# The tail of a two-layer graph kernel: the last tile's flags, the coarse trials of the left-over rows and the end of the last block, on other engines and in another order

## The chip, the cores and the metric

The kernel runs on one core of one Trainium2 chip. The core has five engines with queues of their own: TensorE (PE in the profile, its weight loads PEld), VectorE (DVE), ScalarE (ACT), GpSimd (POOL) and SyncE (SP), which here only issues transfers. Each engine takes its instructions in program order and waits for others by semaphores. The metric is the device time of one execution in microseconds; the median of three runs before the change is 1654.93 us.

## The reference

Two graph layers over 3327 nodes with 256 features, float32. Layer 0 is a graph attention layer with a GRU. Layer 1, where the change lies, runs two steps of a propagation along the adjacency and of an attention in which every row keeps only its largest probabilities, up to a sum of 0.9:

```python
def _top_p_attention(X, W1, W2, W3):
    q = X @ W1.T @ W2.T
    k = X @ W3.T
    probs = jax.nn.softmax(q @ k.T / TAU, axis=-1)
    idx = jnp.argsort(-probs, axis=-1)
    sp = jnp.take_along_axis(probs, idx, axis=-1)
    cs = jnp.cumsum(sp, axis=-1)
    keep_sorted = cs - sp < TOP_P
    mask = jnp.zeros(probs.shape, dtype=bool).at[rows, idx].set(keep_sorted)
    A = probs * mask
    return A / jnp.maximum(A.sum(-1, keepdims=True), 1e-12)

for n in range(2):
    A = _top_p_attention(Xa, W1, W2, W3)
    Xf = R @ Xf                       # R: S + identity, rows divided by their sums
    Xa = A @ Xa
    Z = Z + Xf @ U1[n].T + Xa @ U2[n].T
h = X + Z                             # then a layer norm, + X, and a second layer norm
```

## The kernel before

The rows are worked on in 26 tiles (`NT`) of 128 rows (`P`); the last one has 127 (`TAIL`). Layer 1 keeps all 3327 columns of a tile's logits and probabilities in one row of memory per node. `HALF` is 1664 columns. The second step numbers its tiles from `NT` to `2 * NT - 1`; below they are tile 0 to tile 25 of that step.

**The pipeline of the second step.** All of TensorE, ScalarE, VectorE and GpSimd run in the order in which the program issues the work. For each tile, `run` (L2387) fills seven lists of small jobs, `slots[0]` to `slots[6]`, and `product` (L2343) interleaves them with the tile's own product: group `g` of the masked probabilities is turned (`turn`, TensorE and ScalarE), multiplied (`times`, L2061 on TensorE), and then the jobs of `slots[g]` are issued. While tile `i` is multiplied, tile `i + 1` gets its list of largest probabilities (`list_1`, `list_2`), its flags (`told`), its mask (`mask`) and its neighbours' rows by gathers (`neighbour`), and earlier tiles get their row ends (`tile_end`, six steps each: ScalarE sums, three GpSimd steps, ScalarE normalising, twice over, then a store). `propagate` multiplies the neighbours (`pxf`), `h1` takes their result (ScalarE L1990, GpSimd L1991), and it is stored for later.

**Left-over rows.** A row whose short list of 32 does not settle its bound is flagged. `put_aside_1` and `put_aside_2` count flagged rows, work out a place for each with a small product on TensorE (`pos`), and scatter four numbers a row (`pay`) to a table `left_over` with an indirect DMA that GpSimd issues (L2148). Two blocks of 128 such rows, h0 and h1, are worked out again in full at the end. h0 holds rows of the first 14 tiles, h1 the rest, so h1 can be loaded (`hard_load(1)`, L2158 on SP) only when the last tile's scatter has landed. Then its indices are made (L2161 and L2162), its rows gathered (`hard_gather`, L2176), its queries and logits built (`hard_q`, `hard_exp`).

**A block's bound.** To find which probabilities to keep, a block lowers an upper bound `top` in up to six trials with the factors of `CUTS`. A trial on ScalarE (`coarse_bound`) is four passes (L2231) and eight small steps, on GpSimd; `COARSE` says how many trials of h0 and of h1 go there. A trial on VectorE (`bound`, L2258 to L2263) is one pass over all columns (`kept_sum`, L1963) and three small steps, and the rest of the six go there. Then `hard` sums what lies below `top` (L2273), finds the largest in groups (L1775), sorts a list of 72 (L1794, L1796), settles the bound (L1809 to L2295), drops up to 24 equal values in three passes over all columns (`drop`, L1957) and masks (L2301, one pass). `hard_end` makes the product (`pavh`) and starts the row end.

**The order at the end.** In the last tile's loop h0's coarse trials are finished, its VectorE work (`hard_first`) is put one step into each slot, and h1's load, queries and exponentials go between. After the loop, `ends` issues: the one coarse trial of h1; the rest of h0's work; h0's product; h1's five VectorE trials; h1's `hard`; the final check `whole` (L2523 to L2538), whose result decides if a slow version runs instead; h0's scatter; h1's product; h1's row end; h1's scatter.

Of the kernel before, what the change touches and what calls it, by code (L numbers as in the profile page):

```python
# [16 lines left out]
P = 128  # L17
# [100 lines left out]
COARSE = (4, 1)  # L118
# [1120 lines left out]
class Layer1:  # L1239
# [559 lines left out]
    def settle(self, lst, before, last, thr2, r, drop, flag, tag, room=None):  # L1799
# [19 lines left out]
        engine = nc.vector if room_given else nc.gpsimd  # L1819
# [81 lines left out]
    def list_2(self, i):  # L1901
# [8 lines left out]
            v.lst, before[:r], v.last, v.thr2, r, DROP, self.flag[:r, n, v.at : v.at + 1], tag  # L1910
# [21 lines left out]
    def one_over(self, i):  # L1932

        nc, v = self.nc, self.items[i]
        r = v.r
        nc.gpsimd.tensor_scalar(v.rA[:r], v.thr2[:r], 0.5e-12 / TOP_P, v.sA[:r], ALU.mult, ALU.max)
        nc.gpsimd.tensor_tensor(v.rA[:r], v.rA[:r], self.minus_one[:r], ALU.pow)
# [63 lines left out]
    def moments(self, src, r, tag):  # L2001

        nc = self.nc
        st = self.st.tile([P, nc.vector.BN_STATS_DIM], F32, tag="bn", name=f"bn{tag}")
        nc.vector.bn_stats(st[:r], src)
        mv = self.st.tile([P, 2], F32, tag="mv" + tag[0], name=f"mv{tag}", bufs=4)
        nc.vector.bn_aggr(mv[:r], st[:r])
        nc.gpsimd.tensor_scalar(mv[:r, 1:2], mv[:r, 1:2], 1.0, LN_EPS, ALU.mult, ALU.add)
        nc.gpsimd.tensor_tensor(mv[:r, 1:2], mv[:r, 1:2], self.power[:r], ALU.pow)
        return mv  # L2010

    def sums(self, h, r, tag):
# [7 lines left out]
        yield  # L2020
        sq = self.st.tile([P, 1], F32, tag="sq" + tag[0], name=f"sq{tag}", bufs=2)
# [7 lines left out]

    def shift(self, mv, r, tag):  # L2030
        shift = self.small("shift", f"shift{tag}")
        self.nc.gpsimd.tensor_scalar(shift[:r], mv[:r, 0:1], mv[:r, 1:2], -1.0, ALU.mult, ALU.mult)
        return shift[:r]

    def normalized(self, h, mv, shift, r):
        self.nc.scalar.activation(h, h, AF.Identity, bias=shift, scale=mv[:r, 1:2])
# [35 lines left out]
    def output_rows(self, h, terms, r, tag):  # L2072

        nc = self.nc
        m = self.moments(h, r, f"a{tag}")
        shift = self.shift(m, r, f"a{tag}")
        yield
        self.normalized(h, m, shift, r)
        nc.gpsimd.tensor_tensor(h, h, self.g[:r], ALU.mult)
        for term in terms:  # L2080
            nc.gpsimd.tensor_tensor(h, h, term, ALU.add)
# [274 lines left out]
    def ends(self, first, older, last):  # L2356
# [24 lines left out]
        for _ in self.hard_end(1):  # L2381
            pass
# [224 lines left out]
```

## Time and profile before

| what | value |
|---|---|
| median of three runs (1652.97 to 1655.37) | 1654.93 us |
| the profiled execution | 1656.51 us |
| its span in the profile | 1654.7 us |
| busy: TensorE, VectorE, ScalarE, GpSimd | 86%, 83%, 66%, 63% of the span |
| last tile's own product starts | 1505.9 us |
| h1's pay rows in hand | 1515.6 us |
| h0's first trial on VectorE | 1515.5 us |
| h1's first trial on VectorE | 1563.6 us |
| h1's list pass (L2273) | 1585.4 us |
| h1's mask (L2301) | 1618.5 us |
| h1's product on TensorE | 1623.6 to 1640.3 us |
| last scatter issued | 1649.5 us |

A line of the timeline has the start and the length in microseconds, the engine, the line of the kernel, the operation, what it writes and reads with partitions x elements, and in brackets how long the engine was idle before it and what ended that. In the view of the waits the three numbers are the total in microseconds, how often, and the longest. In the view of the windows each engine has its busy time in the window with the number of its instructions. The chain is the work that ended last, followed back from the last instruction.

### The profile page before, as it was taken

The page shows a single profiled execution, that of the slowest core. Times are in us where ns is not written, and L with a number is a line of the kernel's source. Part 1 is how long each engine was busy: PE and PEld are TensorE (multiplying, and loading weights), DVE is VectorE, ACT ScalarE, POOL GpSimd, SP SyncE. Part 2 cuts the span into 40 slices and gives each one's busy share as a digit, 9 for nine tenths or more (in the row PEclk, how much of TensorE's full clock was granted, in tenths as well). Part 3 has the DMA queues.
Part 4 walks back from the last instruction along what each step waited for, and adds up shares of the span by engine and source line. Part 5 has one row for each costly group of instructions (what it writes and reads, how often), then busy time and mean ns, then how long its engine had stood idle before and what let it go on. Part 6 is the DMA issues. An engine that isn't in the chain of part 4 may idle for free. (4 is left out here: it accounts for less than half of the span.)

```text
span 1654.7 us, 27171 instructions
## 1 busy us (share of the span) xinstructions
PE 1416.5 (86%) x7743; PEld 968.0 (59%) x7743; DVE 1367.8 (83%) x4873; ACT 1097.3 (66%) x2685; POOL 1045.5 (63%) x1523
## 2 busy tenths in 40 slices
PE   4899999986889999999988799999999999985514
PEld 3756666553555555565554477777777667664413
DVE  5799999537788888888862899999999999985992
ACT  4478888655687888788853566766766677764511
POOL 0366666604576677767753468888888878787331
PEclk7599999996799999999997899999999999997767
DMA  8977776313344344444441122222222222211000
GB/s 260 325 246 257 256 258 169 82 53 105 99 124 125 110 121 120 132 111 121 119 125 49 36 60 62 66 72 69 74 71 71 67 59 72 65 53 29 21 4 5
DMA packets 101637, 178.80 MB, mean 108 GB/s; under 512 B 25976, under 2 KB 64119, under 8 KB 101479
## 3 DMA queue, kind: packets, MB, share of 16 engines
q0 software_dynamic: 26288, 73.75, 17.4%
q1 hardware_dynamic: 61818, 93.49, 17.2%
q10 hardware_dynamic: 13372, 9.76, 1.8%
q8 instruction: 63, 1.03, 0.3%
q14 instruction: 96, 0.78, 0.2%
HBM read 139.92 MB, written 37.07 MB: 107 GB/s over the span
## 5 line engine op out<-in xcount | busy, mean ns | idle before, releaser
L2061 PE MATMUL pav<-xu,at 128*128 128x256 f32 (+2 forms) x1352 | 339.2, 396 | 21.9 <-ACT at L2047 21.9
L2061 PEld LDWEIGHTS pav<-xu,at 128*128 128x128 f32 (+2 forms) x1352 | 249.4, 194 | 114.7 <-issue 43.4
L1762 ACT COPY array<-pl 128x416 f32<-128x416 f32 (+3 forms) x402 | 184.1, 512 | 127.8 <-PE pl L1759 127.6
L1775 DVE MAX8 cand<-array 128x8 f32<-128x104 f32 (+5 forms) x1233 | 260.5, 286 | 9.5 <-ACT array L1762 9.1
L1759 PE MATMUL pl<-kT,qT 64*128 64x416 f32 (+3 forms) x804 | 204.4, 567 | 9.4 <-ACT array L1762 8.3
L667 POOL DMA_INDIRECT g<-x_rows,edge x130 | 137.0, 1054 | 46.1 <-issue 32.5
L667 POOL DMA_INDIRECT g<-whx,edge x130 | 135.3, 1041 | 46.9 <-issue 37.3
L2047 ACT COPY at<-pt 128x512 f32<-128x512 f32 (+2 forms) x182 | 95.4, 539 | 103.7 <-PE pt L2045 103.6
L667 POOL DMA_INDIRECT g<-y_rows,edge x130 | 137.1, 1054 | 37.0 <-issue 36.0
L1598 POOL DMA_INDIRECT g<-x1k,uidx x130 | 136.9, 1053 | 33.8 <-issue 25.0
L935 DVE FIND_INDEX8 at<-ones,array 128x8 uint32<-128x840 f32 (+1 forms) x104 | 105.9, 1027 | 0.0
L1759 PEld LDWEIGHTS pl<-kT,qT 64*128 64x128 f32 (+1 forms) x804 | 66.6, 187 | 65.6 <-issue 43.8
L1695 POOL TENSOR_TENSOR x<-x,c 128x256 f32<-128x256 f32 (+1 forms) x26 | 18.5, 714 | 84.6 <-ACT c L1690 84.6
L1656 PE MATMUL pav<-g,w 128*128 128x257 f32 (+1 forms) x260 | 64.1, 395 | 3.5 <-DVE w L1650 3.5
L1052 PE MATMUL acc<-g,m 128*128 128x258 f32 (+1 forms) x260 | 63.2, 391 | 0.0
L1986 PE MATMUL pxf<-g,m 128*128 128x256 f32 (+1 forms) x260 | 62.1, 386 | 0.0
L1052 PEld LDWEIGHTS acc<-g,m 128*128 128x128 f32 (+1 forms) x260 | 50.6, 195 | 18.4 <-issue 6.9
L1884 DVE SCALAR_TENSOR_TENSOR cand<-ec,high 128x256 f32<-128x256 f32 (+1 forms) x104 | 56.9, 547 | 2.8
L2094 POOL TENSOR_TENSOR h<-h 128x256 f32<-128x256 f32 (+1 forms) x26 | 55.3, 2127 | 2.0
L691 PE MATMUL pq<-xtq,wkqk 128*128 128x128 f32 (+1 forms) x208 | 36.0, 298 | 23.2 <-ACT xtq L683 16.1
L1656 PEld LDWEIGHTS pav<-g,w 128*128 128x128 f32 (+1 forms) x260 | 48.9, 196 | 10.7 <-DVE w L1650 4.0
L1079 PE MATMUL prz<-wih,hT 128*128 128x512 f32 (+1 forms) x104 | 52.4, 627 | 3.2 <-ACT hT L1072 1.5
(552 smaller groups left out, 3787.9 us busy)
## 6 DMA issues: line engine op xcount, KB each, us to landing
array<-in_adj_dram SPq DMA_DIRECT2D x25, 1248.0 KB
array<-in_adj_dram SPq DMA_DIRECT2D x25, 415.5 KB
members<-m SPq DMA_DIRECT2D x26, 320.0 KB
m<-members SPq DMA_DIRECT2D x26, 320.0 KB
x_rows<-x ACTq DMA_DIRECT2D x25, 128.0 KB
x1k<-x ACTq DMA_DIRECT2D x25, 128.0 KB
xb_rows<-xb SPq DMA_DIRECT2D x25, 128.0 KB
y_rows<-y SPq DMA_DIRECT2D x25, 128.0 KB
```

The costliest lines, as they stand in the source:

```text
L667: self.nc.gpsimd.indirect_dma_start(out=dst[:, b, :], out_offset=None, in_=table[:, :], in_offset=bass.IndirectOffsetOnAxis(ap=self.edge[: ...
L935: nc.vector.max_index(at[:r, g, :], self.ones8[:r], ad[:r, g, :])
L1052: nc.tensor.matmul(acc[:r, : self.WH], m[:, :r], g[:, k, :], start=(k == 0), stop=(k == EB - 1))
L1598: nc.gpsimd.indirect_dma_start(out=v.g2[:, b, :], out_offset=None, in_=sh.x1k[:, :], in_offset=bass.IndirectOffsetOnAxis(ap=v.idx[:, b : b ...
L1656: nc.tensor.matmul(v.acc[:r, : D + 1], v.w[:, b, :r], v.g2[:, b, : D + 1], start=(b == 0), stop=(b == UB - 1))
L1759: nc.tensor.matmul(pl[:r, :w], q[on], self.sh.kT[on, n, s : s + w], start=True, stop=True)
L1762: nc.scalar.copy(l[:r, h * HALF + s : h * HALF + s + w], pl[:r, :w])
L1775: self.nc.vector.max(cand[:r, g * 8 : g * 8 + 8], src[:r, g * group : min(N, (g + 1) * group)])
L1884: nc.vector.scalar_tensor_tensor(v.cand[:r], ec[:r], high[:r, j : j + 1], ec[:r], ALU.is_ge, ALU.mult, accum_out=above[:r, j : j + 1])
L1986: nc.tensor.matmul(acc[:r, :D], v.m[:, b, :r], v.g[:, b, :], start=(b == 0), stop=False)
L2047: nc.scalar.copy(at[:, :full, :r], pt[:, :full, :r])
L2061: nc.tensor.matmul(v.acc[: v.r, :D], at[:k, j - 4 * g, : v.r], V[:k, j, :], start=(j == 0), stop=(j == NT - 1))
```

## The change

It touches only the end of the second step.

- `settle`, `put_aside_1`, `one_over`: the last tile's flag steps, counting and 1/sum move from GpSimd to VectorE, 1/sum of the tile before also. The scatter of the last tile is issued ahead of its mask.
- `COARSE` goes from (4, 1) to (3, 3): three trials on ScalarE and three on VectorE for each block. h1's indices and small trial steps move from GpSimd to VectorE. Its exponentials and its first trial are issued in slots 4 to 6, its trials between the steps of h0's `hard`.
- Three of the last tile's five neighbour gathers move into its own loop, its `propagate` to slot 5; the row ends of the two tiles before the last are put off.
- The block's mask runs in two halves. `whole` moves into h1's product.
- `last_rows` replaces `output_rows` for h1: VectorE does the scaling, adding and normalising; the sum of bias and `x1` is made ahead on GpSimd.

```diff
-COARSE = (4, 1)
+COARSE = (3, 3)
...
-    def settle(self, lst, before, last, thr2, r, drop, flag, tag, room=None):
+    def settle(self, lst, before, last, thr2, r, drop, flag, tag, room=None, alone=False):
...
-        engine = nc.vector if room_given else nc.gpsimd
+        engine = nc.vector if room_given or alone else nc.gpsimd
...
         v.settled = self.settle(
-            v.lst, before[:r], v.last, v.thr2, r, DROP, self.flag[:r, n, v.at : v.at + 1], tag
+            v.lst, before[:r], v.last, v.thr2, r, DROP, self.flag[:r, n, v.at : v.at + 1], tag,
+            alone=(i == STEPS * NT - 1),
...
-        nc.gpsimd.tensor_scalar(v.rA[:r], v.thr2[:r], 0.5e-12 / TOP_P, v.sA[:r], ALU.mult, ALU.max)
-        nc.gpsimd.tensor_tensor(v.rA[:r], v.rA[:r], self.minus_one[:r], ALU.pow)
+        if i + 2 < STEPS * NT:
+            nc.gpsimd.tensor_scalar(v.rA[:r], v.thr2[:r], 0.5e-12 / TOP_P, v.sA[:r], ALU.mult, ALU.max)
+            nc.gpsimd.tensor_tensor(v.rA[:r], v.rA[:r], self.minus_one[:r], ALU.pow)
+        else:
+            nc.vector.scalar_tensor_tensor(v.rA[:r], v.thr2[:r], 0.5e-12 / TOP_P, v.sA[:r], ALU.mult, ALU.max)
+            nc.vector.reciprocal(v.rA[:r], v.rA[:r])
...
+        junk = self.work.tile([P, D], F32, tag="own", name=f"junk2{tag}", bufs=2)
...
+        engine = nc.vector if t == NT - 1 else nc.gpsimd
         flag = self.flag[:, 1, t : t + 1]
         flag16 = self.small("flag16", f"flag16_{t}", dtype=BF16)
-        nc.gpsimd.tensor_copy(flag16, flag)
+        engine.tensor_copy(flag16, flag)
...
-        nc.gpsimd.tensor_scalar(v.far, flag, -1.0e6, self.base, ALU.mult, ALU.add)
+        engine.tensor_scalar(v.far, flag, -1.0e6, self.base, ALU.mult, ALU.add)
...
-        nc.gpsimd.tensor_copy(v.pay[: v.r, 0:1], self.sh.rowid[: v.r, t : t + 1])
-        nc.gpsimd.tensor_scalar(v.pay[: v.r, 3:4], v.lim[: v.r], v.t[: v.r], None, ALU.max)
+        engine.tensor_copy(v.pay[: v.r, 0:1], self.sh.rowid[: v.r, t : t + 1])
+        engine.tensor_scalar(v.pay[: v.r, 3:4], v.lim[: v.r], v.t[: v.r], None, ALU.max)
...
-        nc.gpsimd.tensor_copy(v.idx[:, 0:1], v.pay[:, 0:1])
-        nc.gpsimd.tensor_scalar(v.idx[:, 1:2], v.pay[:, 0:1], float(N - 1), None, ALU.min)
+        engine = nc.vector if k else nc.gpsimd
+        engine.tensor_copy(v.idx[:, 0:1], v.pay[:, 0:1])
+        engine.tensor_scalar(v.idx[:, 1:2], v.pay[:, 0:1], float(N - 1), None, ALU.min)
...
-        xt = self.transposed((v.x[:, 0, :],), P, f"q{v.tag}")
+        xt = self.transposed((v.x[:, 0, :],), P, f"q{v.tag}", "at" if k else "xt")
...
+        engine = nc.vector if k else nc.gpsimd
         less = self.small(f"less{k}", f"less{v.tag}")
-        nc.gpsimd.tensor_scalar(less, v.pay[:, 2:3], 0.5 * (1.0 - 1e-5), None, ALU.mult)
+        engine.tensor_scalar(less, v.pay[:, 2:3], 0.5 * (1.0 - 1e-5), None, ALU.mult)
         for j, f in enumerate(cuts):
             tag = f"{v.tag}_{f}"
             minus = self.small(f"minus{k}", f"minus{tag}")
-            nc.gpsimd.tensor_scalar(minus, v.top, -f, None, ALU.mult)
+            engine.tensor_scalar(minus, v.top, -f, None, ALU.mult)
...
             nxt = self.small(f"top{k}", f"top{tag}")
-            nc.gpsimd.tensor_tensor(nxt, up, v.top, ALU.mult)
+            engine.tensor_tensor(nxt, up, v.top, ALU.mult)
...
+        halves = self.small("sA2", f"sA2{tag}", 2)
+        for h in range(2):
+            p = v.p[:, h * HALF : min(N, (h + 1) * HALF)]
+            nc.vector.scalar_tensor_tensor(p, p, t, p, ALU.is_ge, ALU.mult, accum_out=halves[:, h : h + 1])
         sA = self.small("sA", f"sA{tag}")
-        nc.vector.scalar_tensor_tensor(v.p, v.p, t, v.p, ALU.is_ge, ALU.mult, accum_out=sA)
+        nc.vector.tensor_tensor(sA, halves[:, 0:1], halves[:, 1:2], ALU.add)
...
-        v.end = (self.output_rows if k else self.by_sums)(v.h, [self.b, x1], P, v.tag)
-        next(v.end)
+        if k:
+            v.end = self.last_rows(v, x1)
+        else:
+            self.scaled(v.tag)
+            v.end = self.by_sums(v.h, [self.b, x1], P, v.tag)
+            next(v.end)
+    def last_rows(self, v, x1):
+        nc = self.nc
+        h = v.h = self.work.tile([P, 2, D], F32, tag="xt", name=f"h{v.tag}", bufs=3)[:, 0, :]
+        nc.gpsimd.tensor_tensor(x1, x1, self.b, ALU.add)
+        nc.vector.scalar_tensor_tensor(h, v.acc[:, :D], v.rA, v.h1, ALU.mult, ALU.add)
+        for tag in "ab":
+            st = self.st.tile([P, nc.vector.BN_STATS_DIM], F32, tag="bn", name=f"bn{tag}{v.tag}")
+            nc.vector.bn_stats(st, h)
+            mv = self.st.tile([P, 2], F32, tag="mv" + tag, name=f"mv{tag}{v.tag}", bufs=4)
+            nc.vector.bn_aggr(mv, st)
+            nc.gpsimd.tensor_scalar(mv[:, 1:2], mv[:, 1:2], 1.0, LN_EPS, ALU.mult, ALU.add)
+            nc.gpsimd.tensor_tensor(mv[:, 1:2], mv[:, 1:2], self.power, ALU.pow)
+            nc.vector.tensor_scalar(h, h, mv[:, 0:1], mv[:, 1:2], ALU.subtract, ALU.mult)
+            if tag == "a":
+                nc.vector.tensor_tensor(h, h, self.g, ALU.mult)
+                nc.vector.tensor_tensor(h, h, x1, ALU.add)
+        yield
...
-        open_ends = [older, last]
+    def ends(self, first, open_ends):
...
-        for _ in self.coarse_bound(1, CUTS[: COARSE[1]], self.items["h1"].other):
+        coarse = self.coarse
+        for _ in range(COARSE[1]):
+            for _ in range(4):
+                next(coarse)
+            for _ in range(2):
+                next(first, None)
+            next(coarse, None)
             more()
...
-        self.whole()
         while open_ends:
             more()
         self.hard_store(0)
-        for _ in self.hard_end(1):
+        product = self.hard_end(1)
+        next(product)
+        self.whole()
+        for _ in product:
             pass
         for _ in self.items["h1"].end:
...
-                slot(1, next, beside, None)
-                slot(2, next, beside, None)
+                slot(1 if i + 1 < total else 5, next, beside, None)
+                slot(2 if i + 1 < total else 5, next, beside, None)
...
                     slot(0 if late else 3, self.put_aside_2, i)
                     if late:
                         slot(1, next, aside)
-                        slot(2, next, aside, None)
-                        slot(3, self.mask, i + 1, lambda: self.put_aside_2(i + 1))
+                        slot(1, next, aside, None)
+                        slot(2, self.put_aside_2, i + 1)
+                        slot(3, self.mask, i + 1)
...
-                    slot(g, next, older, None)
-                    slot(g, next, last, None)
+                    if i + 2 < total or late and g == 0:
+                        slot(g, next, older, None)
+                    if i + 1 == total:
+                        if g < 2:
+                            slot(3 * g, next, oldest, None)
+                        slot(g + 4, next, held, None)
+                    if i + 2 < total:
+                        slot(g, next, last, None)
                 if i + 1 < total:
-                    for b, g in enumerate((0, 0, 0, 3, 3) if late else (0, 0, 0, 4, 5)):
+                    for b, g in enumerate((2, 2) if late else (0, 0, 0, 4, 5)):
                         slot(g, self.neighbour, i + 1, b)
+                else:
+                    for b, g in zip(range(2, EB), (2, 3, 4)):
+                        slot(g, self.neighbour, i, b)
...
                     first = self.hard_first()
-                    for g in range(7):
-                        slot(g, next, first, None)
+                    next(first)
                     for _ in range(3):
                         next(load, None)
+                    next(first)
+                    for g in range(5):
+                        slot(g, next, first, None)
                     q = self.hard_q(1)
-                    for g in range(3):
+                    for g in range(2, 5):
                         slot(g, next, q, None)
+                    slot(4, self.hard_coarse)
                     for j, pair in enumerate(self.chunks()):
-                        slot(3 + j, self.hard_exp, 1, pair)
+                        slot((4, 5, 6, 6)[j], self.hard_exp, 1, pair)
...
                 self.product(i, slots)
+                if late:
+                    oldest, held = older, last
...
                 self.items.pop(i - 2, None)
-            self.ends(first, older, last)
+            self.ends(first, [held, older, last])
+    def hard_coarse(self):
+        self.coarse = self.coarse_bound(1, CUTS[: COARSE[1]], self.items["h1"].other)
+        next(self.coarse)
```

`transposed` with a fourth argument takes its tile from the pool named there; `output_rows`, `moments`, `shift` and `normalized` go away.

## The prediction

> **What bounds the kernel now.** The first page gives VectorE 83% and TensorE 86% of the span, averages over stages; the edits lie in the last 180 us, so I read that stretch by windows, then VectorE's waits in it, then the timeline and the chain that ended last.
>
> Busy time of each engine by window:
>
> ```profile
> core 0: us, PE busy (x) PEld busy (x) DVE busy (x) ACT busy (x) POOL busy (x), PEclk, DMA share, GB/s
> 1498.00:1515.00 17.00, 11.57 (x52) 9.46 (x50) 3.83 (x4) 8.69 (x19) 14.95 (x23) 0.88 0.19 32
> 1530.00:1561.00 31.00, 13.60 (x66) 9.09 (x62) 29.78 (x75) 19.04 (x42) 14.10 (x24) 0.77 0.09 26
> 1585.00:1623.00 38.00, 0.00 (x0) 0.00 (x0) 36.64 (x99) 2.51 (x7) 8.24 (x9) 0.50 0.01 3
> ```
>
> From 1515 to 1623 VectorE works almost alone, and from 1585 TensorE does nothing: this stretch lasts as long as VectorE's queue. Just ahead of it, in 1498 to 1515, VectorE is busy for 3.83 of 17 us and GpSimd for 14.95. The view of the waits names both holes:
>
> ```profile
> DVE cndh L2258 <- POOL 0.7071067811865476_19201 L2246: 11.4, 1, 11.4
> DVE idx L2147 <- POOL far L2120: 8.2, 1, 8.2
> ```
>
> The 8.2 us are the last tile's scatter index, which waits for flags that GpSimd works out late; the 11.4 us wait for block h0's fourth coarse trial, whose small steps stand behind everything else in GpSimd's queue. The timeline shows how the second block, h1, gets its rows, and what GpSimd does beside a trial:
>
> ```profile
> 1507.08 2.72 POOL L2148 DMA_INDIRECT left_over<-pay,idx  x1 [0.28 <-issue]
> 1513.03 0.32 SPq L2158 DMA_DIRECT2D payh<-left_over  x1
> 1515.48 3.68 DVE L1963 SCALAR_TENSOR_TENSOR array<-x,cndh 128x3327 f32<-128x3327 f32 x1
> 1515.62 3.59 POOL L2161 CAST idxh<-payh 128x1 uint32<-128x1 f32 x1 [0.36 <-DMA payh<-left_over]
> 1519.78 1.12 POOL L2176 DMA_INDIRECT xh<-xa_rows,idxh  x1 [0.28 <-POOL idxh L2162]
> 1519.83 3.69 DVE L1963 SCALAR_TENSOR_TENSOR array<-x,cndh 128x3327 f32<-128x3327 f32 x1
> 1521.21 3.20 POOL L2176 DMA_INDIRECT xh<-x_rows,idxh  x1 [0.31 <-issue]
> ```
>
> From the scatter's start to its data in hand takes 8.54 us (1507.08 to 1515.62). A trial on VectorE repeats every 4.35 us. A GpSimd step that starts inside a trial ends only behind it (3.59 us for a one-column cast, 3.20 for a gather that else takes 1.0); the gather that started 0.05 us ahead was not held. The last stretch, from the chain:
>
> ```profile
> 1618.48 3.70 DVE qT L2301 x2
> ...
> 1623.48 0.19 PE pb L2537 x2
> 1623.67 1.90 PE pth L2045 x8
> ...
> 1640.35 0.48 ACT hh L2069
> ...
> 1649.79 0.83 POOL out_dram L2326
> ```
>
> One mask, then one product of 17 us, then 9.3 us of handing 256 columns between four engines.
>
> **1. Last tile's flags on VectorE, scatter ahead of the mask.** VectorE ends the list and the gone columns at 1488.1 and now goes on: four flag steps (0.68 us, as the same four took from 1543.31 to 1543.99), six of 0.17, the index 0.16, the two of 1/sum 0.4, some 0.2 for the position product on TensorE: 2.4 us. The drop (3.6) and the mask (3.77) follow without the hole and end at 1497.95 instead of 1503.8. TensorE loses its own 5.5 us wait for the flag, so the last tile's product starts some 7 us earlier. The scatter can issue when GpSimd has added the tile before's rows (L1991). TensorE: position product done at 1489.3, a group of the product 1.9, its transposes 0.5; ScalarE: their copy 0.6, the rows 0.5; GpSimd: the add 0.65 and 0.3 to issue. The scatter starts near 1493.8. The mask starts at 1494.1, so it is a toss-up whether the scatter slips in first. If it does, the pay rows are there at 1493.8 + 8.54 = 1502.35; if it is held like the gather above, between 2 and 4 us later. I take 1.5 later, the middle: 1503.8.
>
> **2. A new wait.** The two index steps of h1 move from GpSimd to VectorE, where they stand ahead of h0's first trial; every trial is queued behind them. VectorE waits from 1498 to 1503.8, then needs 0.35: first trial's cut at about 1504.1, against 1515.29 now.
>
> **3. Three and three.** h0 loses one ScalarE trial (four passes of 1.76, hidden anyhow) and the 11.4 us hole with it; it gains one VectorE trial. With 3 x 4.35 and 0.4 for the last tile's 1/sum, its list pass starts at 1517.5 instead of 1524.0. For h1 three trials run on ScalarE beside h0's lists, and VectorE does their small steps (8 x 0.2 = 1.6) between h0's drops. VectorE: list pass to first drop's end 24.84 now (1524.01 to 1548.85), plus 0.5 for three new small steps: 1542.9; small steps, 1544.5; two drops 8.3, 1552.8; small steps, 1554.4. Then the third trial's four passes on ScalarE, 7.05 and 0.2 of signals, are longer than h0's mask in halves (4.4 with its sums): VectorE waits until 1561.65, and is ready for h1's own trials at 1563.05. Now it is ready at 1563.37, but with five trials ahead instead of three: 2 x 4.35 + 0.3 = 9.0 us won. GpSimd has more row ends left over than now (six steps each of two tiles and three of a third), and a GpSimd step in flight makes VectorE late: masks at 1401.41 and 1474.24 took 4.15 and 4.07 for 3.68. I take 0.6 off: **8.4 us**.
>
> **4. What must be hidden.** h1's exponentials have to end by 1535.4 for the first ScalarE trial to be in time (1542.9 less 7.05 and 0.45). They come behind the last tile's neighbour product on TensorE, now moved to slot 5, which needs three gathers still to be issued. In GpSimd's queue: two gathers for h1, three small steps of an old row end, the three neighbours, with three trials and the list pass (to 1521.2) running. Held as above, about one or two go per trial; the last neighbour goes at 1523.7 and lands 3.6 later (as 1484.12 to 1487.76). The end of the neighbour product 1.0, a pair of logits 1.0, the product's last group 1.1, then twice 1.0 of logits and 1.1 of exponentials in turn, 4.2: 1534.6. It fits by 0.8 us; beyond that, each us costs one us. The row ends put three short passes, some 2 us, on ScalarE between two trials; they lie under VectorE's small steps, and uncovered would cost 2. On SP an old tile's store moves behind h1's load, which waits for nothing new. Renamed small tiles, the second scratch tile and the other pool for h1's transpose cost nothing, being used in order by one engine.
>
> [...]
>
> **5. Mask in halves, checks moved.** TensorE can start on the first half 1.95 us into the mask (half of 3.77, and 0.07) instead of 5.12 (1618.48 to 1623.60): 3.17 won. The final check now sits behind the second group of the product, where TensorE must wait for VectorE's answer: 0.58 from the number to the product that sums it (1622.90 to 1623.48) and 0.27 of signals, 0.85 lost at most. Net **2.3** (1.5 to 3.2).
>
> **6. Last rows' end on VectorE.** From the product's end, 1640.25, to the scatter at 1649.53 takes 9.28 now. New: scaling and adding in one step 0.42 (row L1094, read from the product's memory); twice statistics 0.43, aggregate 0.18, GpSimd 0.19 and 0.56, normalising; two steps of 0.42 (L1101). The normalising step is in no row: between 0.31 (L1389, half as wide) and 0.54 (L1884); I take 0.45. With hand-overs of 0.1 and 0.3 ahead of the scatter: 6.05. **3.2** won (2.5 to 4). The sum of bias and x1 hides under the product on GpSimd; uncovered it would cost 0.7.
>
> **Sum.** 8.4 + 2.3 + 3.2 = 13.9. The profiled execution took 1656.5 (span 1654.7), 1.6 over the runs' median of 1654.93; it would become 1642.6. Against the median: **1641.0**.
>
> **Rivals.**
> - *The scatter is held by the mask to the full* (for it: 3.6 us of mask start 0.3 us behind it; against: the gather at 1519.78 got through): another 2.3 us late, 1643.3. The forecast with either outcome of this toss-up: 0.65.
> - *h1's exponentials come late.* GpSimd's queue is the tight one (14.95 of 17 us busy now); 5 us beyond the slack costs 5: 1646. Against: nothing holds GpSimd between 1521 and 1552. Chance 0.18; with unlisted smaller waits up to 1648.5.
> - *The change doesn't do what it says: the pay load comes no earlier*, because SP's load waited for something other than the scatter. Then VectorE stands at the index steps until 1515.6, everything behind is 11.8 later, and 11.8 of the 13.9 go: 1652.8. Against: the load was issued 5.95 after the scatter's start with nothing else on SP since 1500. Chance 0.07, some of it as part-way cases.
> - *Slower: the same in-order wait, but longer.* It decides from pay rows at 1517.7, 2.1 us later than now, where the gain is used up; at 1523 the time is 1660. It would need GpSimd to reach the scatter only behind mask, gathers and the wait for the add. Chance 0.05.
> - Still faster than forecast (scatter free, no lock losses, all of 3.2 and 4): 17.7 won, 1637.2; chance 0.05.
>
> **How the numbers follow.** A measurement of this kernel tells about 0.2%, 3.3 us. Faster by more: the first two, the last, and the part-way half of the third, 0.90. Within: 0.05. Slower: 0.05. The range runs from the best case, 1637, to the late exponentials with smaller waits, 1648.5.
>
> **What would show it.** Right: VectorE's last mask ends near 1498; the pay load issues near 1500 instead of 1513; h0's first trial starts at 1503 to 1507; three trials with h1's rows, the list pass of h1 near 1576 instead of 1585.4; TensorE starts inside the last mask; the final scatter 6 us behind the product's end. Wrong: a VectorE wait above 8 us at h1's index steps, or at the first small step of h1's trials; ScalarE's exponentials of h1 ending behind 1538; a TensorE hole above 1 us inside the last product.

## The result, and the profile after

The changed kernel took 1636.99 us (median of five, 1634.00 to 1637.64) against 1654.93: a ratio of 0.989, 95% interval 0.9877 to 0.9904. Two later comparisons of the same two kernels gave 0.9911 (0.9891 to 0.9931) and 0.9901 (0.988 to 0.9923): 17.9, 15.4 and 16.9 us. The forecast was 13.9 us, 1641.0, with 1637.0 as its lower end.

The profiled execution took 1634.00 us, its span 1632.2. It is 22.5 us shorter than the profile before, more than the medians say, because it is 6.2 us ahead at tile 24's first transposes (1472.57 against 1478.79), where the change has done nothing yet; 5.8 of them are there already at the second step's first mask (923.9 against 929.7). From there to the end it takes 159.6 us instead of 175.9: 16.3 won in the tail. Of these, 10.7 lie ahead of h1's mask (forecast 8.4), 1.9 between the mask's start and the first use of the finished product (2.3), 3.4 between that and the last scatter (3.2), and 0.35 behind it. So the miss lies in the first stretch. The profile after is told by the steps of the forecast; to set a time of it beside one of the profile before, add 6.2.

The windows of the changed kernel, over the stretches that answer to those before (the first starts just behind the last tile's mask, the third goes from h1's list pass to its mask):

```profile
core 0: us, PE busy (x) PEld busy (x) DVE busy (x) ACT busy (x) POOL busy (x), PEclk, DMA share, GB/s
1491.00:1508.00 17.00, 14.29 (x76) 11.58 (x75) 12.38 (x15) 4.75 (x10) 13.75 (x6) 0.90 0.17 32
1523.00:1554.00 31.00, 3.73 (x14) 2.15 (x12) 26.64 (x66) 28.41 (x48) 10.82 (x15) 0.56 0.03 9
1568.00:1602.00 34.00, 3.30 (x17) 2.54 (x15) 32.72 (x92) 6.18 (x19) 11.56 (x18) 0.60 0.04 11
```

VectorE is busy for 12.38 of the first 17 us (3.83 before). Its hole has moved and shrunk. In 1523 to 1554 ScalarE now works as long as VectorE (28.41, it was 19.04): these are h1's three trials. The view of the waits, VectorE from 1465 on:

```profile
DVE hh L2310 <- PE pavh L2048: 8.9, 1, 8.9
DVE number L2557 <- PE total L2555: 5.3, 1, 5.3
DVE idxh L2134 <- DMA payh<-left_over: 4.5, 1, 4.5
DVE bothh_0.5_19584 L2211 <- ACT array L2205: 2.9, 1, 2.9
```

The first two are VectorE standing by while TensorE makes the last product, and cost nothing by themselves. The holes of 11.4 and 8.2 us are gone. In their place are the wait in order for h1's pay rows (4.5) and the one for the third ScalarE trial (2.9). Both were foreseen, at 5.85 and 2.85. The timeline shows where the forecast's toss-up fell:

```profile
1487.00 3.71 DVE L1928 SCALAR_TENSOR_TENSOR p<-p,t 127x3327 f32<-127x3327 f32 x1
1487.05 2.62 POOL L2120 DMA_INDIRECT left_over<-pay,idx  x1 [0.26 <-DVE p L1962]
1492.66 0.32 SPq L2130 DMA_DIRECT2D payh<-left_over  x1
1495.31 0.15 DVE L2134 CAST idxh<-payh 128x1 uint32<-128x1 f32 x1 [4.53 <-DMA payh<-left_over]
1495.62 3.68 DVE L1968 SCALAR_TENSOR_TENSOR array<-x,cndh 128x3327 f32<-128x3327 f32 x1
1496.27 3.92 POOL L2149 DMA_INDIRECT xh<-xa_rows,idxh  x1 [2.54 <-PE pt L2032]
1500.49 4.06 POOL L2149 DMA_INDIRECT xh<-x_rows,idxh  x1 [0.30 <-issue]
```

The scatter started 0.05 us behind the start of the mask and was not held: 2.62 us, as the 2.72 before. The two gathers, which started 0.65 and 0.51 into a trial, were held to its end (3.92 and 4.06). Between the scatter and the pay rows lie 8.26 us. SP's load follows the scatter's start by 5.61 us (5.95 before), so the rival that the load waits for something else falls. The end of the chain:

```profile
1612.31 0.19 PE pb L2562 x2
...
1618.97 2.61 PE pavh L2048 x12
...
1621.60 0.50 DVE hh L2310
...
1623.73 0.42 DVE hh L2318
...
1627.64 0.80 POOL out_dram L2326
```

ScalarE and the long way over four engines are gone from it: VectorE takes every step of 256 columns, and GpSimd only the small steps of the two powers and the scatter. The final check (`pb`) now stands inside the product.

### The profile page after: what moved, and what is told of

It reads as the page before. It is cut to its first block, busy times and chain, and to the rows that moved or that the text cites. A ratio compares the mean times of both kernels' runs of the same rounds, so it can differ in the third digit from the quotient of the medians.

```text
span 1632.2 us, 27188 instructions
## 1 busy us (share of the span) xinstructions
PE 1417.1 (87%) x7743; PEld 968.2 (59%) x7743; DVE 1372.3 (84%) x4921; ACT 1103.0 (68%) x2690; POOL 1036.5 (64%) x1484
## 5 line engine op out<-in xcount | busy, mean ns | idle before, releaser
L1695 POOL TENSOR_TENSOR x<-x,c 128x256 f32<-128x256 f32 (+1 forms) x26 | 18.5, 712 | 81.7 <-ACT c L1690 81.7
L1052 PEld LDWEIGHTS acc<-g,m 128*128 128x128 f32 (+1 forms) x260 | 50.6, 195 | 18.4 <-issue 7.4
L2065 POOL TENSOR_TENSOR h<-h 128x256 f32<-128x256 f32 (+1 forms) x26 | 58.6, 2253 | 2.0
```

The costliest lines, as they stand in the source:

```text
L1052: nc.tensor.matmul(acc[:r, : self.WH], m[:, :r], g[:, k, :], start=(k == 0), stop=(k == EB - 1))
```

## The experiments

**How they are compared.** The stretch ahead of the change differs from execution to execution: tile 24's first transposes came at 1472.6 to 1481.4 us in the first six profiles, in no order that goes with the code. The last eight runs were on another chip, where everything ahead of the second step took some 100 us longer (its first mask came at 1025.8 to 1033.6 us, against 923.9 and 929.7); the second step itself took the same (the changed kernel from that mask to the end of the span: 707.7 there, 708.3 in its first profile). So the verdicts go by stretches within one profile. The pivot is the start of the last tile's mask, because all steps behind it hang on it (all in us):

| kernel | scatter's start against the mask's | scatter takes | index steps behind the mask's start | h0's list pass to h1's | mask to h1's mask | mask to end |
|---|---|---|---|---|---|---|
| before | +6.96 | 2.72 | +15.50 | 61.37 | 118.36 | 154.6 |
| changed | +0.05 | 2.62 | +8.31 | 59.82 | 114.59 | 145.2 |
| changed, again | +0.05 | 2.62 | +7.45 | 59.53 | 113.43 | 144.5 |
| changed, third | +0.08 | 2.62 | +7.24 | 59.62 | 113.31 | 144.5 |
| one copy ahead of the scatter | +0.12 | 6.05 | +11.42 | 59.85 | 117.73 | 148.7 |
| later gather | +0.22 | 5.96 | +11.54 | 59.65 | 117.65 | 147.4 |
| later scatter | +4.86 | 2.62 | +12.00 | 60.34 | 118.78 | 148.9 |
| earlier scatter | -1.02 | 2.61 | +6.09 | 59.72 | 112.72 | 143.4 |
| three and two trials | +0.05 | 2.62 | +7.33 | 59.22 | 113.01 | 144.3 |
| earlier scatter, three and two | -0.80 | 2.61 | +6.44 | 59.65 | 112.73 | 142.7 |
| earlier scatter, four and two | -2.70 | 2.60 | +4.45 | 60.86 | 108.02 | 138.8 |
| earlier scatter, five and two | -3.57 | 2.60 | +3.67 | 63.85 | 110.18 | 141.2 |

**The changed kernel again, and a third time.** No edit.

> The changed kernel once more, unchanged. In the first pair of profiles the changed kernel was 6.2 us ahead at tile 24's first transposes (1472.6 against 1478.8 us), before any work that the change touches there, and its tail from there to the end took 159.6 us against 175.9. Theory A (the 16.3 us of the tail are the change, the 6.2 us ahead of it differ from run to run): the median is again 16 to 18.5 us below the kernel before, the tail is 159 to 160.5 us, and tile 24 starts anywhere between 1472 and 1480 us. Rival B (something in the change, such as the second scratch tile of the row ends or other addresses in memory, makes the stretch ahead faster as well): tile 24 starts near 1472.6 again, and near 1478.8 in every kernel without that.

> The changed kernel unchanged, beside the two versions below, and once more a look at where its scatter falls. Theory A: last mask's start to the end takes 144 to 145.5 us if the scatter starts up to 0.05 us behind the mask's start, and 147.5 to 149 if it starts 0.1 or more behind; which of them comes depends on a tenth of a microsecond, so both may show up among executions of the same kernel. The median is 15 to 18 us below the kernel before.

Medians 1637.78 (before, on the same chip: 1653.22) and 1737.59 (1754.52). Tile 24 started at 1475.5 in the first of them, with 159.0 us to the end. Kernels with the same code up to there started it at 1477.5, 1480.0 and 1481.4. So rival B falls: what was ahead in the first profile was not the change. Why it differs stays open; nearly all of it lies ahead of the second step (above). Both tails lie where A put them, with the scatter 0.05 and 0.08 behind the mask's start.

**The scatter later.** Its instruction goes to slot 3, behind the neighbours' gathers; its index stays early (`True` leaves the scatter out of `put_aside_2`, and `put_aside_3` issues it; the split itself is not shown).

```diff
-                        slot(2, self.put_aside_2, i + 1)
+                        slot(2, self.put_aside_2, i + 1, True)
+                        slot(3, lambda v=self.items[i + 1]: self.put_aside_3(v, v.aside))
```

> The changed kernel with one edit: the last tile's scatter is issued in slot 3 behind the mask, and behind the neighbours' gathers of slot 2 on GpSimd, instead of in slot 2; its flags and index are still made early on VectorE. Theory A (the pay rows set when VectorE can take h1's index steps, and everything behind stands in line): the scatter starts some 4 us later (a mask of 3.7 us holds it), VectorE's wait at the index steps grows from 4.5 to 8 to 10 us, and the time is 3.5 to 6 us above the changed kernel. Rival C (ScalarE's trials for h1, which VectorE meets at their third sum with a wait of 2.9 us, set the pace): the wait at the index steps grows the same, but 2 to 3 us of it are given back at that third sum, so the time is 0 to 3 us above. Rival D (the wait in order is hidden): no change.

```profile
DVE idxh L2142 <- DMA payh<-left_over: 8.2, 1, 8.2
...
DVE bothh_0.5_19584 L2219 <- ACT array L2213: 2.9, 1, 2.9
DVE bothh_0.0625_19493 L2219 <- ACT array L2213: 1.0, 1, 1.0
```

VectorE's waits in this kernel: the wait for the pay rows grew from 4.5 (3.7 in the second profile) to 8.2, and nothing was given back at the third sum, which is 2.9 in both. Mask to end grew by 3.7 and 4.5 us, the median to 1643.97, 6.2 above the changed kernel's 1637.78. A holds; C and D fall. The new wait of 1.0 at the *first* sum is the forecast's rival of the late exponentials in small: here they ended 18.75 us behind the start of h0's list pass (17.3 in the changed kernel).

**The scatter earlier.** The whole of it goes to slot 1, ahead of the tile before's addition on GpSimd (L1996).

```diff
-                        slot(2, self.put_aside_2, i + 1)
+                        slot(1, self.put_aside_2, i + 1)
```

> The changed kernel with one edit: the last tile's scatter is issued in slot 1, ahead of the addition of the tile before's rows on GpSimd, instead of in slot 2. Theory A: the scatter starts 2 to 3 us earlier, at about 1484.5 of the first profile's clock, the index steps and h0's first trial come as much earlier, and the time is 2 to 3 us below the changed kernel. Rival C (h1's trials on ScalarE set the pace): the first trial is earlier by the same, the wait of 2.9 us at the third sum grows by it, and the time does not move. A third outcome: mask or scatter hold each other, and the mask ends later by what the scatter gained.

```profile
1494.55 2.61 POOL L2120 DMA_INDIRECT left_over<-pay,idx  x1 [2.08 <-issue]
1495.57 3.69 DVE L1928 SCALAR_TENSOR_TENSOR p<-p,t 127x3327 f32<-127x3327 f32 x1
1497.13 2.70 POOL L1996 TENSOR_TENSOR h<-h,x 128x256 f32<-128x256 f32 x1
```

It started 1.02 us ahead of the mask, not 2 to 3: it stood for 2.08 us behind the scatter of the tile before, in a wait whose releaser the profile does not show. The addition behind it was now held by the mask (2.70 instead of 0.72). Mask to end is 143.4, between 1.1 and 1.8 below the three changed profiles. The median, 1636.49, cannot be told from 1637.78. A's direction holds, at half its size.

**h1's rows gathered later.** The gather that only the block's end needs goes to slot 6.

```diff
-                    for _ in range(3):
+                    for _ in range(2):
                         next(load, None)
...
+                    slot(6, next, load, None)
```

> The changed kernel with one edit: the gather of h1's rows of x (4.06 us on GpSimd, held by a trial on VectorE, needed only in the block's end) is issued in slot 6 instead of between the gather of xa and the row ends. Theory C (GpSimd's queue sets when ScalarE can go on: it waited 5.5 us for the row end's small steps behind that gather; so h1's exponentials and its three ScalarE trials come late, and VectorE waits 2.9 us at the third sum): exponentials end 3 to 4 us earlier, that wait shrinks to under 0.5 and the time falls by 2.5 to 3 us. Rival E (the third trial is late because its four passes of 1.8 us start only after VectorE's small steps of the second, not because the exponentials are late): the exponentials end earlier, the wait stays, and the time does not move.

```profile
DVE idxh L2134 <- DMA payh<-left_over: 7.8, 1, 7.8
...
DVE bothh_0.5_19584 L2211 <- ACT array L2205: 2.9, 1, 2.9
```

The wait at the third sum stayed at 2.9. The exponentials ended 16.9 us behind the start of h0's list pass, against 17.3 and 17.7: 0.4 to 0.8 earlier instead of 3 to 4. So C falls and E holds: that wait is the third trial's four passes against a shorter mask. The other wait was the surprise: the code ahead of the gather is the same, yet the scatter started 0.22 behind the mask's start, took 5.96, and the pay rows came 3 to 4 us later. The median is 1640.75, 3.0 above the changed kernel's, and the intervals of the two ratios overlap.

**One copy ahead of the scatter.** To see whether that tenth decides:

```diff
+        if i + 1 == STEPS * NT:
+            nc.gpsimd.tensor_copy(self.small("nudge", "nudge"), self.base)
         nc.gpsimd.indirect_dma_start(
```

> The changed kernel with one instruction more: GpSimd copies a single column (0.2 us) just ahead of the last tile's scatter. In two profiles of the changed kernel the scatter started 0.05 us behind the start of the mask on VectorE and took 2.62 us; in the run with the later gather, which differs only behind it, it started 0.22 us behind the mask's start and took 5.96. Theory A (a GpSimd step that starts early enough gets through, one that starts a little later is held to the mask's end, and the pay rows set the pace): the scatter starts 0.3 us into the mask, takes 5.9 to 6 us, the index steps come 3.3 to 3.7 us later against the mask's start, and from there to the end nothing changes, so the stretch from the last mask's start to the end grows from 144.4 or 145.2 us to 148 to 149. Rival F (5.96 was a chance of that run): the scatter takes 2.6 us and the stretch grows by no more than 0.3 us.

```profile
1590.17 0.18 POOL L2121 COPY nudge<-base 128x1 f32<-128x1 f32 x1
1590.43 3.68 DVE L1928 SCALAR_TENSOR_TENSOR p<-p,t 127x3327 f32<-127x3327 f32 x1
1590.55 6.05 POOL L2122 DMA_INDIRECT left_over<-pay,idx  x1 [0.20 <-DVE p L1962]
1600.27 0.32 SPq L2132 DMA_DIRECT2D payh<-left_over  x1
1601.85 0.15 DVE L2136 CAST idxh<-payh 128x1 uint32<-128x1 f32 x1 [7.67 <-DMA payh<-left_over]
```

The scatter started only 0.12 behind the mask's start, and that was enough: it ended 2.5 us behind the mask's end, as if begun there. The index steps came 4.2 us later than in the changed kernel's profile on the same chip, and mask to end grew by 4.2 (144.5 to 148.7). The medians, 1740.93 and 1737.59, come from two comparisons in which the kernel before itself took 1759.26 and 1754.52, so they do not show it. Rival F falls. Five profiles now lie on two sides: 0.05, 0.05 and 0.08 free, 0.12 and 0.22 held. With three and two trials, below, it is 0.05 again and free.

**Two ScalarE trials for h1 instead of three**, alone and with the earlier scatter.

```diff
-COARSE = (3, 3)
+COARSE = (3, 2)
```

> The changed kernel with h1's third trial back on VectorE (COARSE 3 and 2). In the profile of the changed kernel VectorE waits 2.9 us for ScalarE's passes of that trial and then needs 2.1 us for its small steps; a trial of its own takes 4.36. Theory A (VectorE's queue from the pay rows to h1's list pass is all that counts): 5.0 less and 4.4 more, so the stretch from h0's list pass to h1's list pass, 59.5 to 59.8 us in all runs so far, falls by 0.6 us and the time does not move measurably: the third ScalarE trial bought nothing. Rival G (a trial on ScalarE is a trial saved, as the forecast of two times 4.35 us had it): the stretch grows by 2 to 4.4 us.

> Both the earlier scatter (slot 1) and two ScalarE trials for h1. Theory A: the stretch from tile 24's first transposes to the end, 159.6 and 159.0 us in the two profiles of the changed kernel and 157.6 with the earlier scatter, becomes 156.5 to 157.5; the time is 1.5 to 2.5 us below the changed kernel. If the two gains do not add, because the row ends left over on GpSimd hold VectorE elsewhere, it stays near 158.

The stretch from list pass to list pass was 59.22 and, with the earlier scatter, 59.65, against 59.53 to 59.85 with three and three (60.34 in the run with the later scatter). It did not grow by 2 to 4.4 us, so G falls: a third trial on ScalarE bought nothing. The gain of 0.6 that A adds shows in one of the two profiles only. The waits of VectorE, with the scatter where it was, have no line for a sum any more:

```profile
DVE hh L2310 <- PE pavh L2048: 9.0, 1, 9.0
DVE number L2557 <- PE total L2555: 5.8, 1, 5.8
DVE idxh L2134 <- DMA payh<-left_over: 3.6, 1, 3.6
DVE array L1962 <- POOL gone L1953: 3.1, 1, 3.1
```

With the earlier scatter, tile 24's first transposes to the end took 157.3 us, within A's range, though 1 us of it is a shorter product (below): from the last mask to h1's mask this kernel is only 0.3 shorter than with three and two alone. The ratios to the kernel before were 0.9869 (0.9837 to 0.99) and 0.9895 (0.987 to 0.992). These overlap with the changed kernel's, so that either is faster than it is likely by the stretches but not shown by the times.

**Four and five ScalarE trials for h0**, in the kernel with the earlier scatter and two for h1. The passes get one more place in five of the earlier tiles' loops. The cut shows four; the other kernel has (5, 2).

```diff
-COARSE = (3, 2)
+COARSE = (4, 2)
...
-                    for g in (0, 2, 5) if i + 3 < total else (0, 1, 2, 5, 6):
+                    for g in (0, 2, 4, 5) if i + 3 < total else (0, 1, 2, 5, 6):
```

> Earlier scatter, two ScalarE trials for h1, and a fourth one for h0, whose passes get one more place in five of the earlier tiles' loops, where ScalarE has room, so that the trial is done before the last tile. Theory A (VectorE's queue from the pay rows to h1's list pass sets the time): one VectorE trial of 4.36 us less than with three and two; the stretch from tile 24's first transposes to the end, 157.3 us there, becomes 152.5 to 153.5, and the time is 5 to 7 us below the changed kernel. Rival H (the earlier tiles' loops are as long as ScalarE allows): the second step's masks come later by up to 1.8 us a tile for five tiles, 9 us in all, and the gain is used up. Rival K (h1's exponentials are late, since VectorE now reaches their first sum sooner): VectorE waits at the first sum, and 1 to 4 of the 4.36 us go.

> The same with five ScalarE trials for h0, one on VectorE. Theory A: 8.7 us less of VectorE's trials than with three and two, but now only h0's mask (4.5 us) lies under the four passes of h1's second trial (7.25 us), so VectorE waits 2.5 to 3 us for its sum: 5.7 to 6.2 us net, the stretch from tile 24's first transposes to the end becomes 151 to 152 us, and the time is 6 to 9 us below the changed kernel. Rival H as above, with 18 us. Rival K: the first sum waits as well, and the time is no lower than with four.

Medians 1749.12 and 1756.03: worse than the changed kernel by 11.5 and 18.4 us. Behind the last mask four trials gained as A says: 112.73 to 108.02 up to h1's mask, though only in part by the trial that is gone, since 2.0 of the 4.7 us come from earlier pay rows. VectorE met no wait at the first sum, so K falls. But the five last masks of tiles came 28.3, 28.9, 22.9, 29.3 and 23.3 us apart (24.7, 22.9, 23.9, 25.8 and 19.2 with three and two), 16.2 us lost. VectorE's waits between 1475 and 1560 say to whom:

```profile
DVE high L1880 <- ACT ec L1870: 9.9, 2, 5.4
```

The next tile's list waits for ScalarE's exponentials, which stand behind the added passes in ScalarE's order; with three and two there is no such line. A third such wait of 4.5 follows behind 1560, which makes 14.4 of the 16.2. So H holds, at nearly double its price. It is the order and not a full engine: in the same stretch ScalarE itself waits 12.7 us for TensorE's transposes. With five, 23.9 us were lost there, VectorE waited 4.2 us for h0's fifth trial and 2.9 at the second sum (2.5 to 3 forecast), and even the stretch behind the last mask was 2.4 us longer than with four.

**The two end parts alone**, in the kernel before, the upper cut in the one and the lower in the other, with `whole` moved. Each ran once, so they go by stretches alone.

```diff
+        if k:
+            v.end = self.last_rows(v, x1)
...
+        for h in range(2):
+            p = v.p[:, h * HALF : min(N, (h + 1) * HALF)]
```

> The kernel before with only the last part of the change: VectorE does the end of h1's rows. Forecast of this part: from the product's end to the last scatter 6.05 us instead of 9.28, 3.2 us won; in the first profile of the changed kernel the same stretch took 5.78, so 3.4 to 3.5 here as well. Rival: the part saves less by itself, because the sum of bias and x1 or the reads of the product's memory are uncovered when the final check still stands ahead of the product: 2.5 us or less.

> The kernel before with only the mask in two halves and the final check behind the second group of the product. Forecast of this part: 2.3 us. In the first profile of the changed kernel the stretch from the mask's start to the first use of the finished product took 20.01 us against 21.87, of which 1.2 us were given back in a longer product. Theory A (the part gives the same alone): 1.8 to 2.2 us won in this stretch. Rival: the longer product came from something else in the changed tail, and alone the part gives 3 us.

`last_rows` alone: 5.79 us from the product's first use to the last scatter (9.18 before), 3.4 won. The halves alone: 19.61 us from the mask's start to that first use (21.87 before), 2.26 won. Both parts give alone what they give in the changed kernel or a little more. The rival of 2.5 us or less falls for the rows. For the halves 2.26 lies just above A's 2.2 and well below the rival's 3, but in one run, and the product that lies in this stretch took 17.1 to 18.5 us from run to run (below); there the rival is unlikely, not excluded.

## Why the prediction was right or wrong

**What failed is the first step: when h1's pay rows are there.** Counted from tile 24's first transposes, the forecast has the last mask at 15.3 us, the pay rows at 25.0 and h0's list pass at 38.7. The first two profiles of the changed kernel show 14.4 and 14.6, 22.7 and 22.0, 36.1 and 35.4. Three terms make it up. The thirteen small steps on VectorE were summed to 2.4 us one after the other; they overlap, and from the first flag step (L1820) to the drop it took 1.8. The toss-up of the scatter was taken at 1.5 us, the middle between a free and a held one; but only the two ends were seen: free 2.62, held 5.96 or 6.05, which puts the index steps 7.2 to 8.3 or 11.4 to 11.5 us behind the mask's start, against the 9.7 of the forecast. And from the scatter to the pay rows it took 7.2 to 8.3 us, where the 8.54 of one row had been taken; the load is issued 5.6 us behind the scatter's start in all three changed profiles, and the rest is its landing, 2.65 us in the first and 1.6 to 1.8 in the others. With the scatter free, the term of 8.4 measures 10.7 and 11.7. That is the whole of the 2.4 and 3.0 us by which the two tails, 16.3 and 16.9 us shorter than before, beat the 13.9; the other terms' errors are under 1 us and cancel.

**The rival that the mask holds the scatter** was priced at 2.3 us on top of the middle. It is real, and the added copy shows it: 4.2 us from free to held, 1.7 from the middle to held. It was not what these three profiles of the changed kernel met, but what stands between is a tenth of a microsecond. The two highest of the changed kernel's eleven times ahead of the change of chip, 1641.3 and 1641.9, may be such cases; without their profiles this stays open.

**The wait in order at the index steps** is what the forecast said: it decides when h0's first trial starts, and a later pay row is a later end. The later scatter and the added copy moved the index steps by 3.7 to 4.6 us and the end by 3.7 to 4.5. The rival that ended slower rested on this mechanism with 13.9 us more of it, and no run came near that.

**Three and three.** From h0's list pass on, the sum was right to its parts: forecast to the second sum of h1 35.3 us, to the third 44.15, measured 35.4 and 44.2; to h1's list pass 59.5 with the 0.6 taken off, measured 59.5 to 59.85 with three and three, but for the later scatter. The 0.6 came as feared: the third trial's small steps took 2.1 instead of 1.4, and the first VectorE trial 3.92 instead of 3.68, both beside GpSimd's row ends; that these made them longer is read from the timeline, not tested. What the forecast did not draw from its own working: the wait it saw at the third sum makes the third trial worthless (three and two: 59.22 and 59.65 us, where three and three took 59.53 to 59.85). Of the "2 x 4.35" for h1 one is enough: with four trials on VectorE and no wait the stretch is as short.

**The exponentials** left 0.9 us in the changed kernel between ScalarE's last pass of the first trial (1533.44) and the step that needs its sum (1534.34; forecast 0.8). In the run with the later scatter they ended 1.4 us later, and VectorE waited 1.0 us. The gathers were held as the forecast had them, 3.92 and 4.06 us, and the exponentials ended 17.3 us behind the start of h0's list pass, where the forecast's sum had 17.1. How far behind a pass's start a GpSimd step was still free was not the same for every step: a scatter 0.08 us behind took its 2.62 us, a flag step that began 0.02 us behind a mask was held (at 1441.98, 3.75 us for 0.29), and another small step 0.02 behind a trial was not (at 1652.94 with the earlier scatter and two trials, 0.19 us). The mask's own time differed too. With the scatter 1.02 us ahead, it took 3.69, against 3.68 in the kernel before. With an addition begun 0.06 ahead, the mask of the tile before the last took 4.06, as the forecast had seen before the change:

```profile
1467.72 0.64 POOL L1996 TENSOR_TENSOR h<-h,x 128x256 f32<-128x256 f32 x1
1467.78 4.06 DVE L1928 SCALAR_TENSOR_TENSOR array<-array,t 128x3327 f32<-128x3327 f32 x1
```

**Mask in halves: 2.3 forecast, 2.26 measured alone, 1.9, 1.4 and 1.3 in the changed kernel.** The spread goes with TensorE's clock. TensorE starts the last product after 32 us of almost nothing, and the mean granted clock of its first 7 us differs between profiles:

```profile
1603.69:1610.69 7.00, 7.00 (x27) 5.92 (x28) 2.59 (x9) 1.76 (x3) 0.00 (x0) 0.64 0.00 0
1613.88:1620.88 7.00, 7.00 (x33) 6.04 (x33) 2.58 (x9) 1.76 (x3) 0.00 (x0) 0.76 0.00 0
```

The first line is the changed kernel, the second the one with the later gather: 27 and 33 matmul instructions in the same 7 us at 0.64 and 0.76. The product lasted 17.9 and 17.1 us. Over all runs of the changed tail it was 17.1 to 18.5, the shortest at 0.77 and the longest at 0.57. What sets the clock was not tested. The final check inside it costs what was put down: TensorE stands idle for 0.66 of the 0.83 us from the start of `total` to `pb` (0.85 at most).

**Last rows' end: 3.2 forecast, 3.4 measured**, alone and together; from the product's first use to the scatter it is 5.78 or 5.79 in every run that has it. The normalising step, which was in no row, took 0.41 (0.45 taken).

**The range** ended at the best case of the tail, 17.7 us, and had nothing for what differs from run to run ahead of the tail. The two tails, 16.3 and 16.9 us shorter, lie inside it, and so do the two later comparisons; that the first median came out 0.01 us below its lower end owes 1.0 to 1.6 us to the stretch ahead, and that is luck. Changed kernels of the same code lay between 1634.0 and 1641.9, so one median of five can be off by more than a microsecond either way: 17.9, 15.4 and 16.9 us for one and the same change.

## What to carry to other kernels

- Where one engine's instruction may or may not be held by another's (the scatter here: 2.62 us free, 5.96 and 6.05 held), a middle between "free" and "held" is a value that no run here showed: find out on which side the start falls, or move the instruction so far that it cannot fall on the wrong one, and give each side its own time in the forecast.
- A wait that a forecast itself puts at an engine's join is work that buys nothing there: check at once what one unit less of it would cost. The third trial was worth nothing to the end, and a fourth one elsewhere cost 16 us, because in that engine's order it stood ahead of work that the next tile waits for.
- Compare tails by stretches from a common mark inside one profile: those of the changed kernel agreed to about 1 us, while whole times of the same kernel on the same chip differed by up to 9 (1648.66 to 1658.07, the kernel before).

## What the runs showed of the hardware that was not expected

- The last tile's indirect scatter was not held when GpSimd started it 0.05 or 0.08 us behind the start of VectorE's mask (two inputs, 127 x 3327): 2.62 us. Started 0.12 behind, it ended 2.5 us past the mask's end and took 6.05 us; 0.22 behind, it took 5.96. A flag step begun 0.02 us behind a mask of 128 x 3327 was held (3.75 us for 0.29).
- The other way, the mask of 127 x 3327 took 3.69 us with a scatter begun 1.02 us ahead of it and 3.68 in the kernel before, where the scatter came 6.96 us behind its start; the mask of the tile before (128 x 3327) took 4.06 with an addition of 128 x 256 begun 0.06 us ahead.
- A `MATCH_REPLACE8` over 3327 columns did not hold GpSimd: the addition L1996 ran beside it in 0.72 us, and beside the mask in 2.70. In the profiles before and after, 57 two-input GpSimd steps of 128 x 256 (`TENSOR_TENSOR`) began inside such a pass and took 0.63 to 0.73 us; 32 began inside a two-input pass over 3327 columns and took 1.89 to 4.04.
- The scatter of the last tile, with 127 rows, took 2.60 to 2.72 us of GpSimd where it was not held; the two of 128 rows just ahead of it in the changed kernel took 1.14 each.
- After 32 to 37 us without work, TensorE's granted clock in the first 7 us of the last product was 0.57 to 0.77 from run to run, and with it the product took 18.5 to 17.1 us.
